# Layer 1's selective scan: dt*x spread through DRAM and copied by ScalarE, more scan inputs made by TensorE, and another order of the work around the scan

## The chip, the core and the metric

The kernel runs on one core of a Trainium2 chip. A core has five engines with a queue each, which work side by side and meet through semaphores: TensorE (PE, matrix products; PEld is its loading of weights), VectorE (DVE), ScalarE (ACT), GpSimd (POOL) and SyncE (SP, which issues DMAs). The metric is the device time of one execution in microseconds (us); three runs of the kernel before gave 939.8, 941.57 and 941.65 us, median 941.57.

## What is computed

Two transformer-like layers over 4 sequences of 256 tokens with 512 features, all in float32 at the interface. Layer 0 is attention plus a gated feed-forward part. Layer 1 is a selective state-space scan plus a routed low-rank part:

```python
def step(h, inp):
    x_t, dt_t, B_t, C_t = inp
    dA = jnp.exp(dt_t[..., None] * A)
    dBx = dt_t[..., None] * B_t[:, None, :] * x_t[..., None]
    h = dA * h + dBx
    y = jnp.einsum('bdn,bn->bd', h, C_t)
    return (h, y)
...
x = x + _L0_attn_ref(xn, ...) + _L0_ffn_ref(xn, ...)
xn = _layernorm(x, axis=-1)
x = x + _L1_attn_ref(xn, ...) + _L1_ffn_ref(xn, ...)
```

For the scan, each sequence has 1024 channels (`d`) with 16 states (`n`) each. Ahead of it come an input projection (x and z), a convolution over 4 tokens with silu, a small projection to dt, B and C with norms, and softplus for dt. Behind it come the gate by silu(z) and the output projection. The low-rank part adds a dense product, and two of eight experts chosen by a router.

## The kernel before

**Tiles and units.** The 1024 channels of a sequence are 8 chunks `c` of 128. A chunk's 128 channels are 4 groups `k` of 32, and one *unit* is one group: 32 channels times 16 states. A unit's tile is 128 partitions by 4 x 256: a partition stands for one of the 32 channels and one of four states `n`, and the free axis has the other state index `g` (4) and the 256 tokens. So a sequence has 32 units, and the four sequences have 128, numbered `u`.

**One unit.** Its work goes over four engines:

- `decays` (line 989, ScalarE): four activations, exp(dt * A), into one of three `decay` tiles. It needs dt of the group spread over the four `n` (`dts`), which goes to DRAM and back by four DMAs a chunk (`spread`, line 956).
- `spread_x` (line 1002, TensorE): dt*x of the group (`du`, made by GpSimd in `step_x`, line 934) is spread over the partitions by a matmul with a 0/1 matrix `sel`. The result `dus` is half of one PSUM tile (`both`, lines 704 and 705); the other half is `ysum`.
- `scan_in` (lines 1009 and 1018): the scan's input `bx` in PSUM, in one of two buffers of pool `psx`. For most units VectorE multiplies the spread B (`brows`) by `dus`. For a group in `ON_PE` TensorE makes it without VectorE: 32 matmuls of a turned dt*x (`dut`, from `step_turn`, lines 943 and 946) with a block-diagonal B (`bdg`). Before the change that is group 0 of every chunk.
- `scan` (line 1027, VectorE): one scan instruction over 4 x 256 elements into a state tile `h`; then GpSimd multiplies it by the spread C (line 1032). Seven state tiles stand in a ring (`NHC`).
- `states_sum` (line 1041, TensorE) adds a chunk's states into `ysum`, after the second unit of the next chunk; `take_sum` (line 1046, VectorE) adds D*x one unit later.

**The order.** The program's order on each engine is the order of the calls; nothing is moved later. The loop over `u` (line 1372) calls, in this order: `first_at`, decays of u+2, the input of u+1, `soon_at` and `at`, `spread_x` of u+2, the scan of u, the sums, `late_at`. All other work of layer 1 (projections `px_mm` and `pz_mm` for the next and this sequence, `conv_in`/`conv_taps`/`conv_out`, `silus`, `pp_mm`, `step` with softplus, `router`, `route`, `dense`, `expert_out`, `out_mm`, loads) is put by hand at units of the scan by `put`, `put_late`, `put_soon` and `put_first` (lines 1267 to 1369). The next sequence's preparation thus lies beside this sequence's scan, and the last third of it (silu, `pp`, softplus, row broadcasts) has its places from unit 20 to 31.

**Memory.** [...] three buffers of pool `psmm` (tag `mm`, shared by all the projections), two double banks of `psx`, and one bank `psy` with `dus` and `ysum`. Weights for the projections come in pieces of 512 KB into three buffers (`w_in`).

Of the kernel before, what the change touches and what calls it, by code (L numbers as in the profile page):

```python
# [17 lines left out]
P = 128  # L18
# [23 lines left out]
def block_kernel(  # L42
# [661 lines left out]
    both = psy.tile([P, 2, S], F32, name="ysum")  # L704
    ysum, dus = both[:, 0, :], both[:, 1, :]
    sel = w1.tile([P, NG - 1, P], F32, name="sel")

    def selection(out, k, n):
        nc.vector.tensor_copy(
            out.rearrange("p k (n j) -> p k n j", n=NG),  # L710
            ident.rearrange("p (k j) -> p k j", j=NB)[:, k : k + n].unsqueeze(2).to_broadcast([P, n, NG, NB]),
        )

    selection(sel, 1, NG - 1)
# [5 lines left out]
    ON_PE = [(0,)] * DC  # L720
# [56 lines left out]
    def mode(b, p, i):  # L777

        if b == 0:
            return "dve" if i == 0 else "act"  # L780
        return "pe" if i == 0 and p < NP - 1 else "act"
# [18 lines left out]
    def conv_in(b, p):  # L800
# [3 lines left out]
        if p == 0:  # L804
            xcs[b] = (act if b % 3 else w1).tile([P, DC, S], F32, tag=f"xc{b % 3}", name="xc")
        pad = pads[p % 2]
        nc.scalar.copy(pad[:, :, KC - 1 :], px)
        for i in range(2):
# [11 lines left out]
    def conv_taps(b, p):  # L820
        pad = pads[p % 2]
        for i in range(2):
# [40 lines left out]
    def pp_square(b):  # L863
        pp = live["pp"]
        sq = four()[:, 0:S]
        nc.scalar.activation(sq, pp[:, 0, :], AF.Square)
        for r in (0, HT):
            mm(pp[r : r + HT, 1, :], lhsT=cst[:64, C_BLK : C_BLK + 64], rhs=sq[:64], start=True, stop=True)
        live["rs"] = four()[:, 0:S]
        inv_root(live["rs"], pp[:, 1, :], eps[:, 1:2])  # L870
# [26 lines left out]
    def rows_bc(b, i):  # L897
        pc, pb = (psmm.tile([P, 2, S], F32, tag="mm", name=n) for n in ("pcr", "pbr"))
        for j in range(2):
            for r, out in ((NB, pb[:, j, :]), (3 * NB, pc[:, j, :])):  # L900
                w = slice(r, r + NB)
                mm(out, lhsT=csel[w, 2 * i + j, :], rhs=nrms[b][w], start=True, stop=True)
        if i == 0:
            crows[b] = odd(b).tile([P, NU, S], F32, tag="cr", name="cr")
            brows[b] = w1.tile([P, NU, S], F32, tag="br", name="br")
        nc.scalar.copy(crows[b][:, 2 * i : 2 * i + 2, :], pc)
        nc.scalar.copy(brows[b][:, 2 * i : 2 * i + 2, :], pb)
# [23 lines left out]
    def step_x(b, c, eng=nc.gpsimd):  # L931

        live["du", c] = w1.tile([P, S], F32, tag="du", name="du", bufs=2)
        eng.tensor_tensor(live["du", c], dts[b][:, c, :], xcs[b][:, c, :], ALU.mult)

    def step_turn(b, c):

        du, n = live["du", c], len(ON_PE[c])
        cols = ident.rearrange("p (k j) -> p k j", k=NG)[:, 0:n, :]
        pt = psmm.tile([P, 4, n, NB], F32, tag="mm", name="ptu")  # L940
        for t in range(4):
            for r in range(2):
                mm(pt[r * HT : (r + 1) * HT, t], lhsT=du[:, t * HT : (t + 1) * HT], rhs=cols,
                   start=True, stop=True)
        dut[b, c] = w1.tile([P, 4, n, NB], F32, tag=f"dut{c % 2}", name="dut")
        nc.scalar.copy(dut[b, c], pt)
# [25 lines left out]
    NHC = 7  # L972
# [26 lines left out]
    def spread_x(u):  # L999
        c, k = u % PER // NU, u % NU  # L1000
        if k not in ON_PE[c]:
            mm(dus, lhsT=sel[:, k - 1, :], rhs=live["du", c], start=True, stop=True)  # L1002

    def scan_in(u):
# [3 lines left out]
        if k not in ON_PE[c]:  # L1008
            nc.vector.tensor_tensor(  # L1009
                bx, brows[b], dus.unsqueeze(1).to_broadcast([P, NU, S]), ALU.mult  # L1010
            )
            return
        i = ON_PE[c].index(k)
        for t in range(4):
            for n in range(NG):
                for r in range(2):
                    w = slice(r * HT, (r + 1) * HT)
                    mm(bx[n * NB : (n + 1) * NB, 2 * r : 2 * r + 2, t * HT : (t + 1) * HT],  # L1018
                       lhsT=dut[b, c][w, t, i], rhs=bdg[w, t, :, n, :],
# [16 lines left out]
    def states_sum(q, ks=range(NG), gs=range(NU)):  # L1036

        hc = [live["hc", q * NU + k] for k in range(NG)]
        for g in gs:
            for k in ks:  # L1040
                mm(ysum[k * NB : (k + 1) * NB, :], lhsT=stack, rhs=hc[k][:, g, :],  # L1041
                   start=(g == 0), stop=(g == NU - 1))

    def take_sum(b, c, w=slice(0, S)):

        nc.vector.scalar_tensor_tensor(
            xcs[b][:, c, w], xcs[b][:, c, w], vec[:, c, V_D : V_D + 1], ysum[:, w], ALU.mult, ALU.add
# [76 lines left out]
    def dense(b, i, k):  # L1124
        if k == 0:
            live["po", b, i] = psmm.tile([P, D], F32, tag="mm", name="po1")
        for hc in (2 * k, 2 * k + 1):
            mm(live["po", b, i], lhsT=xns[b][:, hc, i * P : (i + 1) * P], rhs=late_w["bw"][:, hc, :],  # L1128
               start=(hc == 0), stop=False)

    def expert_out(b, i, stop=False):
        mm(live["po", b, i], lhsT=ident, rhs=x[:, 2 * b + i, :], start=False, stop=False)
        mm(live["po", b, i], lhsT=live["mt"][:, i * P : (i + 1) * P], rhs=late_w["lb"],
           start=False, stop=stop)
# [3 lines left out]

    def reopen(b, i):
        live["po", b, i] = psmm.tile([P, D], F32, tag="mm", name="po2")  # L1140
        mm(live["po", b, i], lhsT=ident, rhs=x[:, 2 * b + i, :], start=True, stop=False)
# [56 lines left out]
    pp_square(0)  # L1198
    pp_norm(0)
# [14 lines left out]
    sel0 = four()[:, 0:P].unsqueeze(1)  # L1214
    selection(sel0, 0, 1)
    pdts = psx.tile([P, NG, S], F32, tag="bx", name="pdts")
    for k in range(NG):
        mm(pdts[:, k, :], lhsT=sel[:, k - 1, :] if k else sel0[:, 0, :], rhs=dts[0][:, 0, :], start=True, stop=True)
# [4 lines left out]
    rows_bc(0, 0)  # L1223
    rows_bc(0, 1)
# [41 lines left out]

    for b in range(B):
        nxt, o = b + 1, 0 if b else 2
        end = nxt == B
        last = 11 if end else 20  # L1270
        if b:
            for c in range(DC):
                put(b, c // 2, out_mm, b - 1, 1, c)
            put_late(b, 3, out_x, b - 1, 1)
            put(b, 6 if end else 20, reopen, b - 1, 0)
            for c in range(DC):
                put(b, (6, 6, 7, 8, 9, 10, 12, 12)[c] if end else (21, 21, 22, 22, 24, 24, 25, 25)[c],
                    out_mm, b - 1, 0, c)
            put_late(b, 13 if end else 25, out_x, b - 1, 0)
        else:  # L1280
            put_late(b, 2, load_z, b, 0)
            put(b, 4, load_z, b, 1)
            put(b, 9, load_late, "rl")
            for k in range(4):
                put(b, 18 + k, load_late, "bw", k, 4)
            put(b, 22, load_late, "lb")
            for k in range(DC):
                put(b, 22 + k, load_late, "ow", k, DC)
# [3 lines left out]
        for c, u in enumerate((1, 3, 4, 6, 7, 8, 9, 10) if end else  # L1292
                              (1, 2, 4, 5, 8, 12, 14, 16) if b else (4, 5, 6, 7, 10, 13, 15, 16)):
            put(b, u, pz_mm, b, c)
            put_late(b, u, pz_copy, b, c)
        for q, u in ((2, 4), (3, 7)) if end else ((2, 4), (3, 10)) if b else ((2, 7), (3, 13)):
            put(b, u, load_z, b, q)
        put_late(b, last, silus, nxt, b)
        for c in range(DC):
            put_late(b, max(4 * c + 6, last + 1 + c), gate, b, c)  # L1300
        for c in range(1, DC):
            put_late(b, 4 * c - 4, step_x, b, c)
            put(b, 4 * c - 2, step_turn, b, c)
        for c in range(2, DC):
            put(b, 3 if c == 2 and not b else 4 * c - 6 + (not b), spread, "dt", b, c)
        if not end:
            put_late(b, 0 if b else 2, norm_stats, nxt)
            put_late(b, 2 if b else 4, norm_scale, nxt)
            put(b, 4 if b else 6, norm_turn, nxt, 0)
            put_late(b, 4 if b else 6, norm_copy, nxt, 0)  # L1310
            put(b, 5 if b else 7, norm_turn, nxt, 1)
            put_late(b, 5 if b else 7, norm_copy, nxt, 1)
            for q in range(NP):
                at_x = ((6, 9, 13, 17) if b else (8, 11, 14, 17))[q]
                put(b, (0, 6, 9, 13)[q] if b else (5, 8, 11, 14)[q], load_x, nxt, q)
                if q == 0:
                    put_late(b, 6 + o, load_dg, nxt, q)
                for i in range(2):
                    put(b, at_x + i, px_mm, nxt, q, i)
                put_late(b, at_x + 1, conv_in, nxt, q)  # L1320
                put_late(b, at_x + 2, conv_taps, nxt, q)
                if q < NP - 2:
                    put_late(b, at_x + 2, load_dg, nxt, q + 1)
                put_soon(b, at_x + 3, conv_out, nxt, q)
            put(b, 21, pp_mm, nxt, 0)
            put(b, 22, pp_mm, nxt, 1)
            put_late(b, 22, pp_square, nxt)
            put_late(b, 23, pp_norm, nxt)
            put(b, 24, softplus_set)
            for q in range(2):  # L1330
                put(b, 24 + q, step, nxt, q)
            put(b, 25, exp_set)
            for i, q in enumerate((0, 2, 1, 3)):
                put(b, 26 + i, step_send, nxt, q)
            put(b, 31, rows_bc, nxt, 0)
            put(b, 31, rows_bc, nxt, 1)
            put_late(b, 26, step_x, nxt, 0)
            put(b, 29, step_turn, nxt, 0)
            put(b, 28, spread, "dt", nxt, 0)
# [173 lines left out]
```

## Time and profile before

| what | us |
|---|---|
| median of three runs | 941.57 |
| the profiled execution's own time | 941.43 |
| its span in the trace | 939.7 |
| layer 0 and start of layer 1 | 0 to 330 |
| first and last scan of layer 1 | 332.2 and 924.6 |

| group in the whole span | count | mean ns |
|---|---|---|
| scan, VectorE, line 1027 | 129 | 2229 |
| states times C, GpSimd, line 1032 | 130 | 2326 |
| bx = br * dus, VectorE, line 1009 | 96 | 1228 |
| decay, ScalarE, line 989 | 504 | 498 |
| spread of du, TensorE, line 1002 | 190 | 436 |
| bx by TensorE, line 1018 | 2048 | 301 |
| table loads, ScalarE, each | | 1283 |

A row of the groups has line, engine, operation, output and inputs with their shapes, count, busy time and mean time of one. A matmul in float32 counts as two instructions in the trace. A row of waits has who waited, on whom, the us in total, how often, and the longest. A "busy" TensorE is not a TensorE at its peak, since matmuls are pipelined.

### The profile page before, as it was taken

How to read it: one execution, taken by the hardware profiler on the slowest of the kernel's cores; microseconds unless marked ns; L12 is line 12 of the kernel's file. 1: busy time of each engine (PE TensorE's matmuls, PEld its weight loads, DVE VectorE, ACT ScalarE, POOL GpSimd, SP SyncE). 2: the span in 40 equal slices, each digit the busy share in tenths (PEclk: the TensorE clock that was granted, in tenths of full speed). 3: DMA queues.
4: the chain of work that ended last, by engine and by line, in shares of the span. 5: the costliest groups of instructions: out<-in, count | busy, mean ns of one | idle time of the engine just before them, and what ended most of it. 6: DMA issues, size and time to landing. Idle time of an engine off the chain costs nothing.

```text
span 939.7 us, 16365 instructions
## 1 busy us (share of the span) xinstructions
PE 806.5 (86%) x6594; PEld 504.3 (54%) x6594; DVE 631.0 (67%) x610; ACT 505.2 (54%) x1020; POOL 461.2 (49%) x375
## 2 busy tenths in 40 slices
PE   5999999999999898996698996887898869786874
PEld 2665556665557566683344774444676434454441
DVE  4587563777344266876766896568698457479884
ACT  4345564355644644757734677653667664346440
POOL 3233320023333034777564699545588644467773
PEclk8899999999999799997687998889999979898997
DMA  6233320012233222352310330140340130121100
GB/s 201 79 113 90 112 79 1 1 45 79 68 107 78 86 68 72 110 173 79 116 55 23 125 102 23 45 145 25 91 134 25 46 101 24 57 69 34 46 1 23
DMA packets 48134, 69.35 MB, mean 74 GB/s; under 512 B 10221, under 2 KB 30457, under 8 KB 47930
## 3 DMA queue, kind: packets, MB, share of 16 engines
q1 hardware_dynamic: 38266, 48.11, 17.5%
q0 software_dynamic: 9072, 18.35, 7.0%
q10 hardware_dynamic: 720, 1.84, 0.6%
q8 instruction: 52, 0.85, 0.4%
q14 instruction: 24, 0.20, 0.1%
HBM read 52.03 MB, written 7.08 MB: 63 GB/s over the span
## 4 chain that ended last, share of the span: by engine, by line
PE 66%; DVE 17%; issue 7%; ACT 5%; POOL 4%; DMA 1%; POOLq 0%; SPq 0%; ACTq 0%; DVEq 0%
DVE h L1027 8%; PE ysum L1041 7%; PE pg L444 6%; PE pu L444 5%; PE po L469 5%; PE px L773 5%; PE ysum L1002 4%; PE po L1144 4%; PE pz L964 4%; PE bx L1018 3%; PE av L397 3%; PE po L1128 3%; DVE bx L1009 2%; PE scT L386 2%; PE pp L860 2%
## 5 line engine op out<-in xcount | busy, mean ns | idle before, releaser
L1032 POOL TENSOR_TENSOR h<-h,cr 128x1024 f32<-128x1024 f32 (+1 forms) x130 | 302.2, 2326 | 225.6 <-DVE h L1027 196.5
L1027 DVE TENSOR_TENSOR_SCAN h<-decay,bx 128x1024 f32<-128x1024 f32 (+1 forms) x129 | 287.3, 2229 | 1.8 <-ACT decay L989 1.8
L989 ACT ACTIVATE decay<-dts,aneg 128x255 f32<-128x255 f32 x504 | 213.1, 498 | 85.3 <-DVE h L1027 77.3
L1009 DVE TENSOR_TENSOR bx<-br,ysum 128x1024 f32<-128x1024 f32 x96 | 117.8, 1228 | 144.7 <-PE ysum L1002 70.2
L456 POOL TENSOR_TENSOR hlo<-g,hhi 128x512 fp32r<-128x512 f32 x28 | 35.9, 1282 | 114.3 <-ACT hhi L455 114.3
L354 DVE TENSOR_REDUCE mpl<-sc 128x4 f32<-128x1024 f32 x64 | 76.7, 1219 | 22.4 <-PE sc L352 20.9
L1002 PE MATMUL ysum<-du,sel 128*128 128x256 f32 x190 | 66.8, 436 | 20.1 <-DVE bx L1009 19.9
L427 POOL DMA_DIRECT2D wgu<-in_wgu x56 | 31.0, 555 | 94.9 <-PE pg L444 93.7
L388 ACT ACTIVATE pe<-scT 128x1024 f32<-128x1024 f32 x64 | 64.0, 1023 | 22.9 <-PE sc L352 14.3
L1144 PE MATMUL po<-ow,xc 128*128 128x512 f32 x128 | 68.8, 661 | 7.6 <-POOL xc L1051 6.7
L1018 PE MATMUL bx<-bdg,dut 64*32 64x128 f32 x2048 | 42.4, 301 | 34.7 <-DVE h L1027 17.4
L1041 PE MATMUL ysum<-h,stack 128*32 128x256 f32 x1024 | 70.2, 416 | 0.0
L1002 PEld LDWEIGHTS ysum<-du,sel 128*128 128x128 f32 x190 | 34.8, 206 | 52.1 <-DVE bx L1009 32.0
L964 PE MATMUL pz<-xn1T,w_in 128*128 128x256 f32 x256 | 61.8, 385 | 0.0
L773 PE MATMUL px<-xn1T,w_in 128*128 128x256 f32 x256 | 61.3, 385 | 0.2 <-ACT xn1T L765 0.2
L1018 PEld LDWEIGHTS bx<-bdg,dut 64*32 64x32 f32 x2048 | 32.3, 115 | 47.3 <-issue 22.0
L964 PEld LDWEIGHTS pz<-xn1T,w_in 128*128 128x128 f32 x256 | 48.7, 192 | 13.9 <-issue 7.0
L773 PEld LDWEIGHTS px<-xn1T,w_in 128*128 128x128 f32 x256 | 47.4, 190 | 7.7 <-ACT xn1T L765 0.6
L444 PE MATMUL pg<-xhi,wgu 128*128 128x512 f32 x112 | 49.6, 443 | 1.4 <-ACT xhi L244 1.4
L1041 PEld LDWEIGHTS ysum<-h,stack 128*32 128x32 f32 x1024 | 32.5, 118 | 34.1 <-issue 18.3
L469 PE MATMUL po<-wd,hhi 128*128 128x512 f32 x112 | 49.4, 441 | 0.0
L452 DVE SCALAR_TENSOR_TENSOR g<-g,pg 128x512 f32<-128x512 f32 x28 | 19.2, 687 | 43.1 <-ACT g L451 43.1
(220 smaller groups left out, 1360.8 us busy)
## 6 DMA issues: line engine op xcount, KB each, us to landing
dts<-dtd SPq DMA_DIRECT2D x124, 128.0 KB, 2.8
wgu<-in_wgu POOLq DMA_DIRECT2D x56, 256.0 KB, 2.7
w_in<-in_inz SPq DMA_DIRECT2D x16, 512.0 KB, 4.3
w_in<-in_inx SPq DMA_DIRECT2D x14, 512.0 KB, 3.9
dtd<-dt SPq DMA_DIRECT2D x16, 256.0 KB, 2.8
wd<-in_wd POOLq DMA_DIRECT2D x7, 512.0 KB, 3.5
ow<-in_ow SPq DMA_DIRECT2D x8, 256.0 KB, 4.7
out<-x SPq DMA_DIRECT2D x7, 256.0 KB, 2.1
```

Source lines behind the costliest of these rows:

```text
L444: mm(ps, lhsT=wgus[i][:, hc, :], rhs=xs[j][:, hc, :], start=(hc == 0 and j == 0), stop=(hc == HC - 1 and j == 1))
L469: mm(po, lhsT=hids[th][j][:, m, i * P : (i + 1) * P], rhs=wd[:, m, :], start=False, stop=(m == MC - 1 and j == 1))
L773: mm(px[:, i, :], lhsT=w[:, i, hc, :], rhs=xns[b][:, hc, :], start=(hc == 0), stop=(hc == HC - 1))
L964: mm(pz, lhsT=w[:, c % 2, hc, :], rhs=xns[b][:, hc, :], start=(hc == 0), stop=(hc == HC - 1))
L989: nc.scalar.activation(da[:, g, 1:], live["dts", b, c][:, k, 1:], AF.Exp, scale=aneg[:, c, k, g : g + 1])
L1002: mm(dus, lhsT=sel[:, k - 1, :], rhs=live["du", c], start=True, stop=True)
L1009: nc.vector.tensor_tensor(bx, brows[b], dus.unsqueeze(1).to_broadcast([P, NU, S]), ALU.mult)
L1018: mm(bx[n * NB : (n + 1) * NB, 2 * r : 2 * r + 2, t * HT : (t + 1) * HT], lhsT=dut[b, c][w, t, i], rhs=bdg[w, t, :, n, :], start=True, sto ...
L1027: nc.vector.tensor_tensor_scan(h[:, n].rearrange("p n t -> p (n t)"), da[:, n].rearrange("p n t -> p (n t)"), bx[:, n].rearrange("p n t -> ...
L1032: (nc.vector if i == NG - 1 else nc.gpsimd).tensor_tensor(h[:, n], h[:, n], crows[b][:, n, :], ALU.mult,)
L1041: mm(ysum[k * NB : (k + 1) * NB, :], lhsT=stack, rhs=hc[k][:, g, :], start=(g == 0), stop=(g == NU - 1))
L1144: mm(live["po", b, i], lhsT=xcs[b][:, c, i * P : (i + 1) * P], rhs=late_w["ow"][:, c, :], start=False, stop=(c == DC - 1))
```

## The change

- **Spread of dt*x.** `sel` and its matmuls go. `step_x` makes `du` (one buffer, not two), `send_x` writes it to DRAM, and `fetch_x` reads the groups that are not in `ON_PE` back, each into all four `n`, by four or eight DMAs a chunk. ScalarE then copies one group at a time into a PSUM bank of its own, `dus`; in the loop this copy stands right behind the decays of the same unit. Only the very first dt (not dt*x) is still spread by matmuls, with a selection matrix in a scratch tile.
- **Sums** go into a buffer of the shared pool, a new one for each chunk; `NHC` is 6.
- **`ON_PE`** is given for each sequence and chunk: 15 units of the first sequence, 12 of the second and third, 19 of the last. `step_turn` turns only the groups needed, up to four.
- **The convolution** by TensorE takes the even chunks 2, 4 and 6, not 0, 2 and 4; `conv_in` and `conv_taps` can do one half.
- **`pp_square`** is split in two, **`rows_bc`** can make B or C alone.
- **`dense` and `expert_out`** are cut into single matmuls, and a block's residual now opens the sum (`open_po`). A sequence's second block stays open over the boundary, as before, and takes the dense part, the experts and the output projection in one sum; the first block's dense part and residual are put back into x, and its experts are added with the output projection, a sequence later.
- **The order** of layer 1's work over the units is written anew.

```diff
-    both = psy.tile([P, 2, S], F32, name="ysum")
-    ysum, dus = both[:, 0, :], both[:, 1, :]
-    sel = w1.tile([P, NG - 1, P], F32, name="sel")
...
+    dus = psy.tile([P, S], F32, name="dus")
...
-    ON_PE = [(0,)] * DC
+    FIRST = ((0, 1, 2, 3), (0, 1), (1,), (0, 1), (1,), (3,), (0, 1), (2, 3))
+    MID = ((0, 1), (2,)) + FIRST[2:]
+    LAST = ((0, 1),) + ((2, 3), (1, 2, 3)) * 3 + ((2, 3),)
+    ON_PE = (FIRST, MID, MID, LAST)
...
-        return "pe" if i == 0 and p < NP - 1 else "act"
+        return "pe" if i == 0 and p else "act"
...
-        live["du", c] = w1.tile([P, S], F32, tag="du", name="du", bufs=2)
+        live["du", c] = w1.tile([P, S], F32, tag="du", name="du")
...
+    def send_x(b, c):
+        live["dud", b, c] = scr.tile([P, S], F32, tag="du", name="dud")
+        nc.sync.dma_start(live["dud", b, c], live["du", c])
+
+    def fetch_x(b, c):
+        t = live["dus", b, c] = act.tile([P, NG - 1, S], F32, tag="dus", name="dus", bufs=2)
+        src = live["dud", b, c].rearrange("(k j) t -> j k t", k=NG)
+        ks, i = ON_PE[b][c], 0
+        for lo, hi in ((0, ks[0]), (ks[-1] + 1, NG)):
+            if lo < hi:
+                for n in range(NG):
+                    nc.sync.dma_start(t[n * NB : (n + 1) * NB, i : i + hi - lo], src[:, lo:hi])
+                i += hi - lo
...
-    NHC = 7
+    NHC = 6
...
     def spread_x(u):
-        c, k = u % PER // NU, u % NU
-        if k not in ON_PE[c]:
-            mm(dus, lhsT=sel[:, k - 1, :], rhs=live["du", c], start=True, stop=True)
+        b, c, k = u // PER, u % PER // NU, u % NU
+        if k not in ON_PE[b][c]:
+            ks = ON_PE[b][c]
+            nc.scalar.copy(dus, live["dus", b, c][:, k if k < ks[0] else k - len(ks), :])
...
+        if ("sum", q) not in live:
+            live["sum", q] = psmm.tile([P, S], F32, tag="mm", name="ysum")
...
-                mm(ysum[k * NB : (k + 1) * NB, :], lhsT=stack, rhs=hc[k][:, g, :],
+                mm(live["sum", q][k * NB : (k + 1) * NB, :], lhsT=stack, rhs=hc[k][:, g, :],
...
+    def open_po(b, i):
+        live["po", b, i] = psmm.tile([P, D], F32, tag="mm", name="po1")
+        mm(live["po", b, i], lhsT=ident, rhs=x[:, 2 * b + i, :], start=True, stop=False)
...
         if 3 <= u < total - 2:
             decays(u + 2)
+            spread_x(u + 2)
...
-        if u + 2 < total:
-            spread_x(u + 2)
         scan(u, 1 if u < total - 1 else 4)
```

The part of the new order that the prediction speaks of, from unit 20 on, for the first three sequences:

```diff
-            put(b, 21, pp_mm, nxt, 0)
-            put(b, 22, pp_mm, nxt, 1)
-            put_late(b, 22, pp_square, nxt)
-            put_late(b, 23, pp_norm, nxt)
-            put(b, 24, softplus_set)
-            for q in range(2):
-                put(b, 24 + q, step, nxt, q)
-            put(b, 25, exp_set)
...
-            put(b, 31, rows_bc, nxt, 0)
-            put(b, 31, rows_bc, nxt, 1)
...
-            put(b, 27, dense, b, 0, 0)
-            put(b, 28, dense, b, 0, 1)
-            put(b, 28, expert_out, b, 0, True)
-            put_late(b, 28, close_x, b, 0)
-            put(b, 29, dense, b, 1, 0)
-            put(b, 30, dense, b, 1, 1)
-            put(b, 30, expert_out, b, 1)
...
+        put(b, 20, open_po, b, 0)
+        many(b, ((21, (0,)), (22, (1, 2))), dense, b, 0)
+        put(b, 22, dense, b, 0, 3, True)
+        put_late(b, 22, close_x, b, 0)
...
+        put(b, 23, pp_mm, nxt, 0)
+        put(b, 24, pp_mm, nxt, 1)
+        put_late(b, 24, pp_square, nxt)
+        put(b, 25, pp_sum, nxt)
+        put_late(b, 25, pp_norm, nxt)
+        put(b, 27, softplus_set)
+        put(b, 27, step, nxt, 0)
+        put_first(b, 28, step, nxt, 1)
+        put_first(b, 28, exp_set)
...
+        put(b, 28, rows_bc, nxt, 0)
+        put(b, 28, rows_bc, nxt, 1)
...
+        put(b, 31, open_po, b, 1)
+        put(b, 31, dense, b, 1, 0)
```

The silus of the sequence stand late in unit 21 (before: 20), the output projection of the former sequence's first block in units 25 to 31 (before: 20 to 25), and `step_x`, `send_x` and `fetch_x` of chunk c late in unit 4c-6, in 4c-5 and in 4c-4.

## The prediction

> **What bounds the kernel now.** I read three views: the page's busy times, then the waits from 330 us to the end (the scan of layer 1 runs there, 610 of 939.7 us; what lies before 330 us is hardly touched), then the same stretch cut into windows and one gap as a timeline.
>
> The busy times show no engine full, TensorE (PE) nearest:
>
> ```profile
> PE 806.5 (86%) x6594; PEld 504.3 (54%) x6594; DVE 631.0 (67%) x610; ACT 505.2 (54%) x1020; POOL 461.2 (49%) x375
> ```
>
> The waits of the scan stage show what VectorE (DVE) waits for before its multiply on line 1009, `bx = br * dus`:
>
> ```profile
> POOL h L1032 <- DVE h L1027: 196.5, 85, 10.8
> ACT decay L989 <- DVE h L1027: 77.3, 53, 3.2
> DVE bx L1009 <- PE ysum L1002: 70.2, 29, 10.2
> DVE bx L1009 <- PE ysum L1041: 68.7, 31, 9.0
> ```
>
> GpSimd (POOL) and ScalarE (ACT) mostly wait for VectorE's scan; VectorE waits 70.2 + 68.7 = 138.9 us for TensorE, always for the spread `dus`: L1002 writes it, and L1041 (the sums) stands with it in one tile and queue. The windows are a stretch inside sequence 1 (14 units) and the passage from it into sequence 2 (18 units); columns: length, busy of PE, PEld, DVE, ACT, POOL, clock, DMA share, GB/s.
>
> ```profile
> 330.00:940.00 610.00, 496.05 (x4901) 311.85 (x4888) 443.14 (x336) 340.79 (x774) 378.67 (x243) 0.90 0.24 69
> ...
> 528.00:579.00 51.00, 45.48 (x540) 33.81 (x540) 46.47 (x31) 37.58 (x91) 43.74 (x30) 1.00 0.27 78
> 579.00:670.00 91.00, 73.00 (x650) 40.73 (x650) 57.45 (x41) 50.38 (x106) 48.85 (x32) 0.87 0.21 65
> ```
>
> Inside a sequence VectorE is 91% busy (46.5 of 51): there it sets the pace. In the passage it is idle 33.5 of 91 us. One gap shows how:
>
> ```profile
> 581.13 1.91 ACT L850 ACTIVATE xc<-xc 128x2048 f32<-128x2048 f32 x1 [2.27 <-POOL xc L832]
> ...
> 583.10 3.68 PE L860 MATMUL pp<-xc,xpw 128*64 128x256 f32 x16 [5.26 <-ACT xc L850]
> ...
> 586.71 1.22 PE L1002 MATMUL ysum<-du,sel 128*128 128x256 f32 x2
> ...
> 590.12 1.23 DVE L1009 TENSOR_TENSOR bx<-br,ysum 128x1024 f32<-128x1024 f32 x1 [9.04 <-PE ysum L1041]
> ```
>
> The next sequence's projection `pp` waits in TensorE's queue for a silu; the spread stands behind it, its first matmuls run slowly after the idle time, and VectorE loses 9.04 us. The same happens behind `pdt` (8.67 us before the multiply at 612.71) and behind `po` (10.2 at most). So the bound is two things: VectorE's own work inside a sequence, and TensorE's queue order in three passages.
>
> **What the Trainium skill says.** "PSUM — Partial Sum Buffer", section "Engine vs sequencer instructions": the queues of ScalarE, VectorE and GpSimd are strictly first in, first out, and matmuls start and complete in program order. The gap above agrees. The same page, "PSUM bank collisions raise a hardware error", has two engines kept apart by bank and quadrant, not by address; `dus` and `ysum` share a bank here, and TensorE waits 32.0 us (weight loads) and 19.9 us (matmuls) at L1002 for the multiply that reads it. "DMA: Bandwidth & Descriptors", "Anatomy of one DMA", gives about 2.0 us fixed; the `dts<-dtd` rows land after 2.8 us, and I use that. "ScalarE: Activation LUTs", "What ACT_TABLE_LOAD costs", gives 1283 ns a load; the trace has 1283 ns.
>
> **The change, part by part.** Times are of the profiled execution (span 939.7, its own time 941.43 us; the median of the three is 941.57, so a difference in span is carried over unchanged).
>
> 1. Removed: 95 spread matmuls (190 instructions, 66.8 us busy = 0.70 each; beside others two passes take 0.43). TensorE: −41 to −67 us. With them goes VectorE's dependence on TensorE's queue in every unit that isn't made by TensorE.
>
> 2. Units made by TensorE rise from 32 to 58 (15, 12, 12, 19 by sequence; before, 8 each). 26 multiplies go from VectorE; between a multiply's start and the next scan's start lie 1.14 us (590.12 to 591.25), so VectorE's path is 26 × 1.14 = 30 us shorter. TensorE gets 26 × 64 instructions, 1.16 us a unit in the timeline (42.4 / 32 = 1.33 by the group): +30 to +34. `step_turn` turns up to 128 columns where it turned 32 (0.66 us now, bound by its weight loads of 0.55); I add 0.15 a chunk, 5 us, at most 10.
>
> 3. Added: 70 ScalarE copies of 128x256 into PSUM. No row shows SBUF to PSUM; the reverse, `sz<-pz`, takes 368 ns. "ScalarE: Activation LUTs", "Step-by-step: what each stage is for", says PSUM is the nearer destination. Lower end: 256 elements at the page's 0.833 ns, 0.21; upper end the softplus row's 474 ns. I take 0.37: +26 us (15 to 33), on an engine busy 341 of 610. Six table loads go (29 to 23 in the program, because the two softplus groups now stand together): −8. The copy waits for the previous multiply (one bank) and stands right behind four decays (1.70 us), which themselves wait for the scan that ends as that multiply begins. It is due when the next scan ends: 1.14 + 2.28 = 3.42 us against 1.70 + 0.37. Cover: 1.3 us; whatever else stands in ScalarE's queue beyond that is charged to VectorE.
>
> 4. Added on the SP queue: 31 sends and 156 fetches. At 0.45 us an issue (four `dts` in 1.81) that is 84 us of a queue with time to spare, but in order. From `du` to a copy's data: issue 0.45, landing 2.8, four issues 1.8, landing 2.8 = 7.9 us. `step_x` stands late in unit 4c−6 and the earliest copy heads unit 4c−2: three units, 10.7 us at 3.56 a unit (14 units from 528.97 to 578.79 us), less GpSimd's lag (its multiply 2.36 and `du` 0.73), plus the 1.7 of decays ahead. Slack about 1.4 us when the first group is needed at once, 5 when one unit later. I charge 5 us in all. A w_in load (512 KB, 4.3 us to land) standing between them can eat it.
>
> 5. Sums rotate through the three shared banks; states keep 6 buffers for 7. Scan 4q+6 now waits for the sums of chunk q, which stand one unit earlier in TensorE's queue. This costs nothing while TensorE lags under one unit (3.5 us) and its lag beyond that otherwise; I take 5 us (0 to 25).
>
> 6. The new order. In the passage: the first half of `pp` stands at unit 23 instead of 21, silu one unit later, softplus in units 27 and 28 in one piece, the row broadcasts at 28 instead of 31; the dense part of the first block goes from units 27 and 28 to 20 to 22, that of the second mostly over the boundary, where VectorE lost up to 4.38 us behind it. Each is the same work in another place, with the DMAs named above.
>
> Sum by place. Inside a sequence, units 8 to 21: four TensorE units before and after, VectorE's 46.5 us stay; 3.9 us of waits for the spread can go, against ScalarE's lag: 0. Passage, units 22 to 39: TensorE units 4 to 8, so VectorE 57.5 − 4.6 = 53 us; ScalarE 50.4 + 3.7 (10 copies) − 2.6 (two table loads) = 51.5, of which silu (two loads, 1.91, 1.89 = 6.4 us) and softplus (two loads, eight activations of 0.39 = 5.7) are solid blocks under which VectorE has two to four units ready. Two engines with 52 us each that hand work to one another don't overlap fully; TensorE's 73 us include matmuls at half speed after idle time. I take 71 us for the 91: −20 in each of three passages, −60. Start of sequence 0: four multiplies fewer in units 0 to 21, but units 0 to 3 wait for layer 0's matmuls: −4. Sequence 3 after the passage: 15 TensorE units for 6, nine multiplies, −10. Together −74.
>
> Cross-check from TensorE: 496 − 41 + 30 + 5 = 490 us; at the 89% it has inside a sequence that is 550 us for the stage, −60; at 92%, 532, −78. The two ways agree; I keep −74: 941.6 − 74 = 867.5.
>
> **The rivals.**
>
> A. TensorE becomes the bound: the same 490 us at 84 to 86% gives 570 to 583 us, −27 to −40, about 908. For: it is the busiest now, takes 26 more units, and each TensorE unit couples the queues again. Against: with nothing of VectorE behind it, its order can slip by units.
>
> B. The wait moves to ScalarE: pad copies and `sz` copies wait there for TensorE (13.4 + 9.3 us now), and decays and copies stand behind them. Half of the 60 from the passages then comes back: 897.
>
> C. Slower: the fetched groups come late. Place: the first copy of a chunk, in ScalarE's queue, where decays and thereby all scans stand behind it. Price: the lateness x on 31 chunks. It decides from 74 / 31 = 2.4 us; at 3.5 us, 867.5 + 108 = 976. For: the slack in 4 is only 1.4 us, and SP waits now up to 21.0 us for decays at `dts`. Against: those waits are SP running ahead, and x = 3.5 means a path of 12.8 us instead of 7.9.
>
> D. The reorder doesn't matter and only the multiplies go: −30, with nothing from the waits: 912. Against: the 9 us gaps are plainly of queue order.
>
> **How the numbers follow.** Forecast (838 to 895): 0.62; A, B and D together, 895 to 935: 0.18; better than 838: 0.06, since VectorE's 443 − 30 leave room; no change: 0.02; C and any other slower way: 0.12. The predicted time is the forecast's, 867. For 8 in 10 the range runs from 838 to 915, leaving out the slower cases, the gains above it and the last part of A to D. Faster by over 0.2% (2 us, about what a measurement can tell): 0.86; same 0.02; slower 0.12.
>
> **What would show it.** Right: waits of the multiply on TensorE gone, the 9 us gaps down to 1 to 4 us behind silu and softplus on ScalarE, passages near 71 us, inner stretches near 51. Wrong: `dus` copies waiting for DMA beyond 2 us each (C); scans waiting for TensorE's `bx` or sums, with PE over 90% in the passage (A); VectorE's multiply waiting for the copy throughout (B); copies far from 0.37 us.

## The result, and the profile after

| kernel | median, us | runs | ratio to before |
|---|---|---|---|
| before | 940.68 | 939.68 to 941.65 | |
| after | 964.36 | 961.36 to 969.42 | 1.0257 [1.0209, 1.0306] |

The change made the kernel 2.6% slower; the forecast was 867 us. The profiled execution of the changed kernel took 969.42 us, the longest of its four; its span is 967.7.

First the page: busy time of each engine in the whole span, with its share and the instructions.

```profile
PE 815.7 (84%) x8068; PEld 509.4 (53%) x8068; DVE 593.5 (61%) x583; ACT 519.1 (54%) x1084; POOL 461.0 (48%) x375
```

VectorE has 37.5 us less to do than before (593.5 for 631.0), as intended, ScalarE 14 us more, and the span is 28 us longer. No engine got fuller, so it is waits that grew. The waits of the changed kernel from 330 us to the end, in the form who, on whom: us in total, times, longest:

```profile
POOL h L1047 <- DVE h L1042: 217.0, 75, 8.7
DVE bx L1024 <- ACT dus L1017: 138.2, 45, 10.3
ACT decay L1003 <- DVE h L1042: 136.3, 55, 5.4
DVE h L1042 <- PE ysum L1058: 53.9, 10, 9.8
...
DVE h L1042 <- PE bx L1033: 13.6, 4, 4.8
```

The multiply's waits on TensorE's spread and sums, 138.9 us together before, are gone. A wait of the multiply on ScalarE's copy stands in their place with almost the same total, 138.2 us, and the scan waits for the sums another 53.9 and for TensorE's `bx` 13.6. Together these are 205.7 us of waits for 138.9; with 37.5 us less work that makes 29 us more on VectorE, near the 28 of the spans. The third line is the other half of the story: the decays wait 136.3 us for VectorE (before: 77.3). Two engines that each wait long for the other can be a sign of a chain that runs around between them.

The timeline shows it. Columns: start, length, engine, line, and in brackets the idle time ahead of the group and what ended it. This is a stretch inside sequence 1 (its units 18 to 20), VectorE (DVE) and ScalarE (ACT) of the changed kernel:

```profile
591.87 2.28 DVE L1042 TENSOR_TENSOR_SCAN h<-decay,bx 128x1024 f32<-128x1024 f32 x1
...
594.18 1.70 ACT L1003 ACTIVATE decay<-dts,aneg 128x255 f32<-128x255 f32 x4 [1.31 <-DVE h L1042]
595.79 0.36 ACT L1017 COPY dus<-dus 128x256 f32<-128x256 f32 x1
...
596.18 1.23 DVE L1024 TENSOR_TENSOR bx<-br,dus 128x1024 f32<-128x1024 f32 x1 [1.66 <-ACT dus L1017]
597.32 2.28 DVE L1042 TENSOR_TENSOR_SCAN h<-decay,bx 128x1024 f32<-128x1024 f32 x1
...
599.63 1.70 ACT L1003 ACTIVATE decay<-dts,aneg 128x255 f32<-128x255 f32 x4 [2.92 <-DVE h L1042]
601.24 0.36 ACT L1017 COPY dus<-dus 128x256 f32<-128x256 f32 x1
...
601.63 1.23 DVE L1024 TENSOR_TENSOR bx<-br,dus 128x1024 f32<-128x1024 f32 x1 [2.04 <-ACT dus L1017]
602.77 2.28 DVE L1042 TENSOR_TENSOR_SCAN h<-decay,bx 128x1024 f32<-128x1024 f32 x1
```

Nothing overlaps here that should. A scan ends, the four decays start (0.03 us later), the copy follows them, the multiply follows the copy, the next scan follows the multiply: 2.28 + 1.70 + 0.37 + 1.14 = 5.49 us by the lengths (the multiply counted to the scan's start), and the scans at 591.87, 597.32 and 602.77 stand 5.45 us apart. With the multiply and the scan alone it would be 3.42.

Why the multiply waits there is in the loop's order, of which the diff moved one line:

```
        if 3 <= u < total - 2:
            decays(u + 2)
            spread_x(u + 2)        # before: behind scan_in(u + 1) and the unit's other work
        if 0 < u < total - 1:
            scan_in(u + 1)
```

`dus` is one tile. The copy for unit u+2 now stands ahead of the multiply of unit u+1, so that multiply has to wait for it. This happens wherever two VectorE units follow each other; by `ON_PE` there are 46 such pairs. In these the multiply also takes the following unit's dt*x, so the changed kernel computes something else there, with operations of the same shapes. The copy in turn stands behind the decays of u+2, which fill the decay tile that the scan of u−1 has just given back, and the scan of u stands behind the multiply in VectorE's queue. So the loop is closed: scan, decays, copy, multiply, scan.

To say where the time went I cut the stage at the 32 starts of `take_sum` (line 1046, after the change 1063), of which none is missing in the records; it stands at unit 6, 10, 14 and so on. "Inner" is unit 6 to 18 of the first three sequences together, "passages" unit 18 to unit 6 of the next, three together; the row of e1 is explained below.

| us | to unit 6 | inner | passages | unit 6 of sequence 3 to the last sum | after it |
|---|---|---|---|---|---|
| before | 371.7 | 136.2 | 322.7 | 101.8 | 7.2 |
| after | 376.9 | 182.0 | 290.6 | 111.4 | 6.8 |
| e1 | 370.0 | 135.3 | 249.6 | 102.2 | 6.7 |

The passages did get shorter, by 32 us. The inner stretches, which the forecast left unchanged, lost 46, the last sequence 10 and the start 5: +28, the difference of the spans.

### The profile page after: what moved, and what is told of

It is laid out like the page before. It is cut to its first block, busy times and chain, and to the rows that moved or that the text cites. A ratio compares the mean times of both kernels' runs of the same rounds, so it can differ in the third digit from the quotient of the medians.

```text
span 967.7 us, 19539 instructions
## 1 busy us (share of the span) xinstructions
PE 815.7 (84%) x8068; PEld 509.4 (53%) x8068; DVE 593.5 (61%) x583; ACT 519.1 (54%) x1084; POOL 461.0 (48%) x375
## 4 chain that ended last, share of the span: by engine, by line
PE 50%; DVE 22%; ACT 12%; issue 6%; POOL 4%; DMA 3%; SPq 2%; ACTq 0%; POOLq 0%; DVEq 0%
DVE h L1042 13%; ACT decay L1003 6%; PE pg L444 6%; PE bx L1033 5%; PE pu L444 5%; PE po L469 4%; PE av L397 3%; PE ysum L1058 3%; PE po L1158 3%; POOL h L1047 3%; DVE bx L1024 3%; PE px L766 2%; PE pz L978 2%; PE scT L386 2%; DVE mpl L354 2%
## 5 line engine op out<-in xcount | busy, mean ns | idle before, releaser
L1042 DVE TENSOR_TENSOR_SCAN h<-decay,bx 128x1024 f32<-128x1024 f32 (+1 forms) x129 | 284.4, 2226 | 66.8 <-PE ysum L1058 53.9
L1003 ACT ACTIVATE decay<-dts,aneg 128x255 f32<-128x255 f32 x504 | 214.0, 497 | 151.7 <-DVE h L1042 136.3
L1024 DVE TENSOR_TENSOR bx<-br,dus 128x1024 f32<-128x1024 f32 x70 | 86.0, 1228 | 138.6 <-ACT dus L1017 138.2
L1033 PE MATMUL bx<-bdg,dut 64*32 64x128 f32 x3712 | 78.1, 304 | 65.5 <-DVE h L1042 49.3
L1033 PEld LDWEIGHTS bx<-bdg,dut 64*32 64x32 f32 x3712 | 59.1, 116 | 94.0 <-DVE h L1042 53.6
L978 PE MATMUL pz<-xn1T,w_in 128*128 128x256 f32 x256 | 70.6, 427 | 4.8 <-ACT xc L806 3.8
L978 PEld LDWEIGHTS pz<-xn1T,w_in 128*128 128x128 f32 x256 | 52.2, 211 | 19.8 <-ACT xc L806 6.2
L766 PE MATMUL px<-xn1T,w_in 128*128 128x256 f32 x256 | 59.0, 384 | 3.4 <-ACT dut L960 2.0
L826 POOL TENSOR_TENSOR xc<-xc,dg 128x256 f32<-128x256 f32 x54 | 39.6, 734 | 19.1 <-ACT dg L811 16.3
L444 PE MATMUL pu<-xhi,wgu 128*128 128x512 f32 x112 | 47.6, 425 | 0.8 <-DVE g L454 0.8
L1158 PEld LDWEIGHTS po<-ow,xc 128*128 128x128 f32 x128 | 24.5, 208 | 41.1 <-issue 25.0
```

The source lines that it names most:

```text
L444: mm(ps, lhsT=wgus[i][:, hc, :], rhs=xs[j][:, hc, :], start=(hc == 0 and j == 0), stop=(hc == HC - 1 and j == 1))
L766: mm(px[:, i, :], lhsT=w[:, i, hc, :], rhs=xns[b][:, hc, :], start=(hc == 0), stop=(hc == HC - 1))
L978: mm(pz, lhsT=w[:, c % 2, hc, :], rhs=xns[b][:, hc, :], start=(hc == 0), stop=(hc == HC - 1))
L1003: nc.scalar.activation(da[:, g, 1:], live["dts", b, c][:, k, 1:], AF.Exp, scale=aneg[:, c, k, g : g + 1])
L1024: nc.vector.tensor_tensor(bx, brows[b], dus.unsqueeze(1).to_broadcast([P, NU, S]), ALU.mult)
L1042: nc.vector.tensor_tensor_scan(h[:, n].rearrange("p n t -> p (n t)"), da[:, n].rearrange("p n t -> p (n t)"), bx[:, n].rearrange("p n t -> ...
```

## The experiments

Three theories stood at the start. T: the order in the loop, that is the copy of u+2 ahead of the multiply of u+1 on a single tile. R: the way of the copy itself (the fetch from DRAM, ScalarE's load), which would be late wherever the copy stands in the loop. S: the sums in rotating banks with six states for seven. The first four kernels ran together, beside 15 runs of the kernel before (941.41 us median); e5 to e8 had seven beside them (939.8), e9 and e10 another seven (939.97). Each ratio is to these.

### e1: the copy behind the multiply

```
         if 3 <= u < total - 2:
             decays(u + 2)
-            spread_x(u + 2)
         if 0 < u < total - 1:
             scan_in(u + 1)
+        if 3 <= u < total - 2:
+            spread_x(u + 2)
```

> The changed kernel with one call moved: the copy of unit u+2 stands behind the multiply of unit u+1, not ahead of it, so each multiply reads its own unit's dt*x again. Theory T (the order of copy and multiply makes a loop scan, 4 decays, copy, multiply of 2.28 + 1.70 + 0.37 + 1.14 = 5.49 us a unit): the multiply's 138 us of waits on the copy fall below 40 us, inner units come every 3.5 to 4 us, time 860 to 905 us. Theory S (the sums and the ring of six states hold the scans): the waits move to scan on sums, above 80 us, time 930 to 955. Theory R (ScalarE is too full or stands behind TensorE in its queue): the multiply's waits on the copy stay above 90 us, time 940 to 965.

Measured: 865.36 us (865.15 to 865.98), ratio 0.9201 [0.9177, 0.9226]. The same instructions as after, one call moved, 99 us less. The waits of this kernel:

```profile
POOL h L1047 <- DVE h L1042: 120.3, 56, 10.6
DVE h L1042 <- PE ysum L1058: 57.9, 11, 11.7
ACT decay L1003 <- DVE h L1042: 38.7, 27, 5.1
...
DVE bx L1024 <- ACT dus L1017: 30.0, 20, 4.9
```

Both halves of the loop shrank together: the multiply's wait from 138.2 to 30.0 us, the decays' from 136.3 to 38.7. The timeline of an inner stretch of it shows the copy where it has time:

```profile
540.57 1.70 ACT L1003 ACTIVATE decay<-dts,aneg 128x255 f32<-128x255 f32 x4 [0.22 <-DVE h L1042]
540.64 1.23 DVE L1024 TENSOR_TENSOR bx<-br,dus 128x1024 f32<-128x1024 f32 x1
541.77 2.28 DVE L1042 TENSOR_TENSOR_SCAN h<-decay,bx 128x1024 f32<-128x1024 f32 x1
542.17 0.36 ACT L1017 COPY dus<-dus 128x256 f32<-128x256 f32 x1
...
544.35 1.22 DVE L1024 TENSOR_TENSOR bx<-br,dus 128x1024 f32<-128x1024 f32 x1
```

The copy at 542.17 lies beside the scan, and the multiply that reads it starts at 544.35 without a wait. T holds. R falls: fetches and copies are the same as in after, and only the place of the copy differs. S's wait is real (57.9 us, in after 53.9), but it is in a kernel that is 99 us faster, so it isn't what made the change slow.

### e2: no copy

The multiply reads the fetched tile in SBUF, of its own unit, and no copy is made:

```
-            nc.scalar.copy(dus, live["dus", b, c][:, k if k < ks[0] else k - len(ks), :])
+            live["dux", u] = live["dus", b, c][:, k if k < ks[0] else k - len(ks), :]
...
-                bx, brows[b], dus.unsqueeze(1).to_broadcast([P, NU, S]), ALU.mult
+                bx, brows[b], live.pop(("dux", u)).unsqueeze(1).to_broadcast([P, NU, S]), ALU.mult
```

> The changed kernel without the copies: the multiply reads the fetched tile in SBUF itself, each its own unit's. T: the loop is gone as in the run with the copy behind the multiply, and 70 copies of 0.37 us leave ScalarE: 850 to 900 us and at most 15 us faster than that run. R: over 25 us faster than that run. S: like that run, waits of scans on sums above 80 us. The multiply may take longer with both inputs in SBUF; at 1.23 us it does not.

Measured: 906.12 us (903.73 to 909.72), ratio 0.9625 [0.9591, 0.9659]. It is faster than after by 58 us, as T would have it, but lies above T's 850 to 900 us, and where T expected up to 15 us less than e1 it is slower by 41, although without a copy there is one thing less to wait for. The groups (after the bar: busy us, mean ns of one, and the idle time before with its releaser) show a longer multiply on both engines, where after and e1 have 1.23 and 2.33 us:

```profile
L1047 POOL TENSOR_TENSOR h<-h,cr 128x1024 f32<-128x1024 f32 (+1 forms) x130 | 327.9, 2533 | 114.8 <-DVE h L1042 109.4
L1024 DVE TENSOR_TENSOR bx<-br,dus 128x1024 f32<-128x1024 f32 x70 | 146.5, 2092 | 4.9 <-DMA dus<-dud 3.5
```

70 multiplies at 0.86 us more are 60 us of VectorE, and the waits on the copy that go (30.0 us in e1) give only part of it back. The fetch is not late (3.5 us in all). Why the multiply is longer, e8 asks.

### e3: the copy ahead of the decays, still ahead of the multiply

```
         if 3 <= u < total - 2:
-            decays(u + 2)
             spread_x(u + 2)
+            decays(u + 2)
         if 0 < u < total - 1:
             scan_in(u + 1)
```

> The changed kernel with the copy of unit u+2 ahead of that unit's four decays but still ahead of the multiply of unit u+1 in the program. As in the changed kernel, where two units of VectorE follow each other, the first is multiplied with the second's dt*x. T: the multiply still waits for the copy, but the copy no longer waits for a scan through the decays; 3.5 to 4 us a unit, 860 to 910 us. S and R: 935 to 970 us, as in the changed kernel.

Measured: 895.9 us (895.57 to 897.96), ratio 0.953 [0.9502, 0.9557]. The copy no longer waits for the scan of u−1 by way of the decays; it is still asked for a unit too early, as in after. The waits of this kernel:

```profile
DVE bx L1024 <- ACT dus L1017: 66.7, 26, 8.8
ACT decay L1003 <- DVE h L1042: 58.8, 40, 4.5
DVE h L1042 <- PE ysum L1058: 54.8, 10, 11.1
```

So the 99 us split: 68 go with the decays out of the loop, 31 more with the copy behind the multiply (895.9 to 865.36). That a ScalarE that lags then has a unit's time to catch up is my reading of the 31. The wrong operand is not what costs time: e3 has it too.

### e4: the kernel before with a ring of six

```
-    NHC = 7
+    NHC = 6
```

> The kernel before with six state tiles in the ring, not seven; nothing else. S: the scan must wait for the sums a unit earlier, as in the changed kernel (53.9 us there): 960 to 995 us. T: the ring costs little by itself, 940 to 955 us.

Measured: 941.08 us (936.74 to 946.59), ratio 0.9994 [0.9971, 1.0017]. One state less costs nothing that this measurement can tell in the kernel before. This tests the ring alone; the rotating banks, the other half of S, stand in e1 as well, which is fast. S falls as the cause.

### e5 and e6: the sums earlier in TensorE's queue

What remains in e1 is the scans' wait for the sums, 57.9 us. e5 calls the sums of a chunk ahead of the unit's other work, e6 does so in unit 29 of each sequence alone. The edit of e5, on top of e1's:

```
+        if u >= 5 and u % NU == 1:
+            states_sum(u // NU - 1)
         for f, a in (*soon_at.get(u, ()), *at.get(u, ())):
             f(*a)
         scan(u, 1 if u < total - 1 else 4)
...
-        if u >= 5 and u % NU == 1:
-            states_sum(u // NU - 1)
```

> Of the first variant (865.36 us) with the sums of a chunk put ahead of the unit's other TensorE work, in every chunk. There, scans wait 57.9 us for the sums (11 times, 11.7 at most), and in the gap at 593.47 us the sums stood behind the row broadcasts, whose copies stood behind softplus. If that queue order is what remains of the passages: those waits under 15 us, 825 to 845 us. If the passage is set by ScalarE and GpSimd, and the sums' place only shows it: the wait moves to the decays or to bx, 855 to 870 us. If the other work, now behind a sum that waits for GpSimd's multiply, is late instead: over 870 us.

> The same move for one chunk of each sequence alone, the one whose sums stand in unit 29 beside the row broadcasts. By the first theory the two or three gaps of 8.4 to 11.7 us fall to 2 to 5, that is 840 to 852 us; by the second 860 to 866 us.

Measured: e5 856.72 us (855.25 to 858.14), ratio 0.9116 [0.9067, 0.9165]; e6 862.02 us (860.48 to 863.43), 0.9167 [0.9125, 0.9209]. Both times lie in the ranges of the second theory. Its sign is not there, though: in e5 the scans' waits on the sums fell only from 57.9 to 42.6 us, and no wait moved to the decays (scans wait 4.9 us for them, in e1 4.8) and little to `bx` (its wait on the copy is 31.8, in e1 30.0). The cut at the sums tells where e5's 8.6 us come from: the passages take 249.9 us (e1: 249.6), the last sequence 92.1 (e1: 102.2). The gap in the passage stayed, in e5 as

```profile
592.42 2.29 DVE L1042 TENSOR_TENSOR_SCAN h<-decay,bx 128x1024 f32<-128x1024 f32 x1 [9.53 <-PE ysum L1058]
```

because the row broadcasts of the unit before still stood ahead of the sums. So the queue order in the passage was not yet tested; e9 and e10 do that.

### e7: fewer units by TensorE

e1 with 39 units made by TensorE for 58:

```
-    ON_PE = (FIRST, MID, MID, LAST)
+    ON_PE = (FIRST[:2] + ((1,),) * 3 + ((3,), (1,), (3,)), *(((0, 1), (2,)) + ((1,),) * 3 + ((3,), (1,), (3,)),) * 3)
```

> Of the first variant with 39 units made by TensorE for 58. By the forecast's step 2 each is worth 1.14 us on VectorE's path: 865 + 19 x 1.14 = 887 us. If TensorE is the bound of the stage (rival A), 19 units of 1.2 to 1.3 us less make it faster: 840 to 845 us. If the units pay on one side what they cost on the other: 861 to 870 us.

Measured: 877.25 us (876.25 to 881.09), ratio 0.9337 [0.9291, 0.9383]: in none of the three ranges, and 11.9 us slower than e1, which is 0.63 us for each of the 19 units. TensorE was busy 14 us less (767.3 for 781.2), and the kernel got slower with it, so TensorE's load isn't the bound, and rival A falls. But a unit is worth a little over half of what step 2 had for it: the passages take 261.3 us for 249.6, the rest together under 4 us more (inner 137.7 for 135.3, last sequence 102.5 for 102.2; the profiled execution was the longest of e7's four). The multiply's waits on the copy rose to 55.5 us (e1: 30.0), while the scans' on the sums fell to 22.7 (57.9).

### e8: e1, with the operand in SBUF

The copy into PSUM is made as in e1, and nobody reads it; the multiply reads the fetched tile:

```
+            live["dux", u] = live["dus", b, c][:, k if k < ks[0] else k - len(ks), :]
+            nc.scalar.copy(dus, live["dux", u])
...
-                bx, brows[b], dus.unsqueeze(1).to_broadcast([P, NU, S]), ALU.mult
+                bx, brows[b], live.pop(("dux", u)).unsqueeze(1).to_broadcast([P, NU, S]), ALU.mult
```

> Of the first variant with nothing changed but where the multiply reads dt*x: the fetched tile in SBUF instead of the copy in PSUM, the copy being made all the same and read by nobody. If two operands in SBUF make the multiply slow, it takes 2.0 to 2.1 us for 1.23, GpSimd's multiply 2.5 for 2.33, and the time is 900 to 915 us. If the slow multiply of the run without a copy came from its earlier start or its place in the order, it takes 1.23 here, and the time is 850 to 866 us, since the wait for the copy (30.0 us) is gone.

Measured: 905.66 us (905.45 to 907.15), ratio 0.9635 [0.9592, 0.9678], the time of e2. The groups (lines are one further down in this kernel):

```profile
L1048 POOL TENSOR_TENSOR h<-h,cr 128x1024 f32<-128x1024 f32 (+1 forms) x130 | 329.9, 2550 | 111.2 <-DVE h L1043 105.9
L1025 DVE TENSOR_TENSOR bx<-br,dus 128x1024 f32<-128x1024 f32 x70 | 143.8, 2054 | 1.3
```

So it is the operand's place, not the order. The timeline of this kernel shows how the time is lost, one operation at a time:

```profile
548.96 1.23 DVE L1025 TENSOR_TENSOR bx<-br,dus 128x1024 f32<-128x1024 f32 x1
549.07 1.70 POOL L932 TENSOR_TENSOR du<-dt,xc 128x256 f32<-128x256 f32 x1
...
550.73 2.35 POOL L1048 TENSOR_TENSOR h<-h,cr 128x1024 f32<-128x1024 f32 x1
552.42 1.76 DVE L1025 TENSOR_TENSOR bx<-br,dus 128x1024 f32<-128x1024 f32 x1
```

At 548.96 VectorE comes first: its multiply takes the usual 1.23 us, and GpSimd's `du`, 0.73 us in e1, takes 1.70. At 552.42 GpSimd is under way until 553.08; the multiply lasts 1.76 us, as if it had begun in earnest at 553. That is what the Trainium skill, "SBUF — State Buffer", section "SBUF: two separate sides", says of the port pair that the two share: a VectorE operation with two inputs in SBUF and a GpSimd operation that reads SBUF exclude each other, and "the other fully blocks". These lines agree with it, and so does the whole trace of e8: 54 of the 70 multiplies begin while a GpSimd operation is under way, and each of them ends 1.09 us after that operation does; the other 16 take 1.22 to 1.24 us. In e1, with the operand in PSUM, 63 begin under one and all take 1.21 to 1.23. So it is the meeting with GpSimd that costs, not SBUF by itself. The copy into PSUM, 0.37 us on ScalarE, spares VectorE 0.83 to 0.86 us a unit.

### e9 and e10: the row broadcasts behind the sums

e5, with the broadcasts of B and C moved from unit 28 to 29 (e9) or 30 (e10):

```
-        put(b, 28, rows_bc, nxt, 0)
-        put(b, 28, rows_bc, nxt, 1)
+        put(b, 29, rows_bc, nxt, 0)
+        put(b, 29, rows_bc, nxt, 1)
```

> Of the variant with the sums first (856.72 us), whose gap of 9.53 us before the scan at 592.42 us stayed, because the row broadcasts of unit 28 still stand ahead of the sums of unit 29 in TensorE's queue and wait there for ScalarE's softplus, decays and copies. Here the broadcasts move to unit 29, behind the sums. If that queue order makes the gap: the sums start when GpSimd's multiply ends at about 583.4 us, the three gaps fall by 5 to 7 us each, 836 to 843 us. If ScalarE's block of softplus and table loads sets the passage and the gap only shows it: waits of the same size on decays, bx or rows take its place, 850 to 858 us.

> The same with the broadcasts in unit 30, one unit further from the softplus block. If the first theory holds and the rows are in time for unit 64: 834 to 845 us. If the rows come late for the first units of the next sequence, whose GpSimd multiply reads them: a new wait of 2 to 5 us in each of three passages and 845 to 858 us.

Measured: e9 868.03 us (866.49 to 869.18), ratio 0.923 [0.9216, 0.9244]; e10 855.64 us (854.77 to 856.52), 0.9102 [0.9087, 0.9117]. The move did what it was to do, and the time didn't follow: the first theory's 834 to 845 us were not met. In the same passage e9 has the first of these lines, e10 the other two:

```profile
603.72 2.35 DVE L887 TENSOR_TENSOR bdg<-eye,pbt 128x1024 f32<-128x1024 f32 x2 [10.65 <-PE pbt L881]
```

```profile
586.80 2.29 DVE L1042 TENSOR_TENSOR_SCAN h<-decay,bx 128x1024 f32<-128x1024 f32 x1 [4.77 <-PE ysum L1058]
...
595.38 2.35 DVE L887 TENSOR_TENSOR bdg<-eye,pbt 128x1024 f32<-128x1024 f32 x2 [5.92 <-PE pbt L881]
```

The gap of 9.53 us before the scan is halved (4.80 us in e9, 4.77 in e10). In e10 5.92 us appear ahead of the block-diagonal B (`bdg`), whose matmuls (`pbt`) stand behind the broadcasts in TensorE's queue; in e9 that gap is 10.65 us, and its time is above what either theory gave. From the `take_sum` of unit 54 to that of unit 66 e5 takes 54.6 us, e9 59.6, e10 54.8. Against e5, VectorE's waits for the sums fall by 20.2 us in e9 and 14.5 in e10, and those for `pbt` rise by 25.7 and 13.0. So shifting one member moves the wait. It did not move to the decays, `bx` or rows, as the other theories had it; that the block of softplus, table loads, decays and row copies as a whole holds the passage is my reading, and no run takes that block away. Which order would be best is left open; e10 and e5 are the best found, 9% under before, with 1.1 us between them and ranges that overlap.

## Why the prediction was wrong

**The step that failed is 3.** It had the copy "due when the next scan ends: 1.14 + 2.28 = 3.42 us against 1.70 + 0.37. Cover: 1.3 us." That is the cover in the order of before, with the copy behind the multiply of u+1. In the changed loop the copy stands ahead of that multiply, and the multiply is due at once when the scan of u−1 ends: the cover isn't 1.3 us but −2.07, the 1.70 of the decays and the 0.37 of the copy. For the 46 pairs that is 95 us, an estimate from these lengths; e1, without the loop, is faster by 99. The durations in the step were right (copy 0.364 us for 0.37, decays 1.70). What wasn't asked is which instruction is the next to need the tile that the copy writes. What it needed was all there: `dus` is a single tile, the diff puts `spread_x` right behind the decays, and the loop has the input of u+1 behind these. e1, with that one call behind the multiply again, runs at 865.36 us, against the forecast's 867.

**The sum of the rest, tried on e1.** By places, e1 against before, in the cut of the table:

- Inner stretches: taken 0, measured −0.9.
- Passages: taken −60, measured −73.
- Start: taken −4, measured −1.8.
- Last sequence: taken −10, measured +0.4. There scans wait 25.1 us for the sums (before: 14.2 for the spread and the sums); e5, with 15.7, gets the 10 us.

So the total of −74 was met by e1 (−76) with two terms off by 13 and 10 us in opposite ways: that it came so close is in part luck.

**The other steps.** Step 1: TensorE's busy time in the stage fell more than thought, 496 to 471 us in e1 for 490; but busy time is no fixed amount of work, for with the same instructions it is 505 us in after. (The slow matmuls after idle time that the sum by places counts are in the trace of before: the matmuls of `pp` start in pairs 0.44 us apart from 583.10 on, after 5.3 us of idle TensorE and at a granted clock of 0.50, and 0.22 us apart from 592.29 on, without idle time and at 1.00.) Step 2: VectorE's work fell by 38 us, 26 x 1.23 = 32 of it the multiplies, but in e7 a TensorE unit moved the end by 0.63 us, not 1.14; by the waits of e7 and e1 part of what VectorE saves becomes waiting for the sums (22.7 and 57.9 us). Step 4: 5 us were charged for late groups; all copies together wait 1.2 us for DMA in after and 1.5 in e1. The slack of 1.4 to 5 us was enough. Step 5: 5 us taken (range to 25); the waits are 53.9 and 57.9 us, and what taking the sums forward gave was less than the wait it removed: in e5 15.3 us less waiting and 8.6 us less time, in e10 29.8 and 9.7. Step 6: the passages are where e1's gain is, but no run separates the new order from the spread that left TensorE's queue, so what the order alone brings is not shown.

**The rivals.** B named the right wait, the multiply on ScalarE's copy, but as a load on ScalarE in the passages, at 30 us; the sign under which it was to be known ("VectorE's multiply waiting for the copy throughout") is what the profile showed. C, the case on the slower side, gave the right sign by a mechanism that isn't there. A fell with e7, though its sign, scans that wait for the sums, is in e1 (57.9 us, with TensorE busy 88% of the passages). D, −30 from the multiplies alone, fell with e1.

## What to carry to other kernels

When a producer of a single buffer is moved in a program that keeps its order, ask two things before any duration: which reader comes next after it, and what the producer itself stands behind. If the reader was queued earlier in the loop and now comes later, and the producer stands behind work that itself waits for the reader's engine, there is a cycle through both engines, and its length is the sum of everything on it; add that sum up before crediting any overlap. The sign of it in this profile was two large waits of about the same total that point at each other, and a step between iterations (5.45 us) that nearly equals the sum of the lengths (5.49).

## What the runs showed of the hardware

I had not expected that leaving out a copy costs time. A float32 multiply of 128x1024 on VectorE took 1.23 us with one operand in PSUM and 2.05 to 2.09 us on average with both in SBUF while GpSimd worked beside it, and GpSimd's own multiply went from 2.33 to 2.53 or 2.55 us. Only multiplies that met a GpSimd operation were longer. In this kernel that is 40 us (865.36 against 905.66); the copies that avoid it keep ScalarE busy for 26 us in all.
